# Implicit filters of two layers computed first on 128 partitions, and a thinner spread of the last eight channels' Haar work

## The chip, the cores and the metric

The kernel runs on one core of a Trainium2 chip. The metric is the device time of one execution in microseconds; each figure shown is a median of runs, and a profiled execution gives the trace that the text reads. TensorE does the matrix products, VectorE and ScalarE the elementwise work and the copies out of PSUM, and the queues of SyncE (SP) and ScalarE (ACT) issue all the transfers.

## The reference

Four layers follow each other on an input of 4 images, 64 channels, 256 x 256 pixels. Layers 0, 1 and 3 are long two-dimensional convolutions, one filter a channel, whose filter is the outer product of two vectors, `hx` and `hy`. Each vector comes from a small network:

```python
def _implicit_filter(z, w1, b1, w2, b2, w3, b3, wo, freq, t, deltas):
    h = jnp.sin(freq * (z @ w1 + b1))
    h = jnp.sin(freq * (h @ w2 + b2))
    h = jnp.sin(freq * (h @ w3 + b3))
    h = h @ wo
    return h * jnp.exp(-t * jnp.abs(deltas))
...
k = jnp.einsum('ijk,imk->ijmk', hx, hy)[0]        # one 256 x 256 filter a channel
y = irfft2(rfft2(x, 512) * rfft2(k, 512) / 512)[..., :L, :L]
out = y + x * bias[:, None, None]
```

`z` has 256 positions and 33 features, the hidden width is 64 and the output has one value a channel. So a layer needs two such networks, one an axis.

Layer 2 works in a Haar basis: a forward two-dimensional Haar transform, a scaling, a 64 x 64 mix of the channels, a soft threshold (twice, summed), the inverse transform, and the input added:

```python
f1 = haar2d(x)
for i in range(2):
    f4 = jnp.einsum('bchw,oc->bohw', f1 * v[i], conv_w[i])
    acc = acc + jnp.sign(f4) * relu(jnp.abs(f4) - tau[i])
y = haar2d(acc, inverse=True) + x
```

## The kernel before

**Convolutions as products.** Since a filter is separable, a convolution is a Toeplitz product from the left and one from the right. `contract` (lines 164 to 168) does one of them: four fp32 products of a 128 x 128 piece of the image with a piece of a Toeplitz matrix `t`. The Toeplitz matrix is not computed: `toeplitz` (line 155) loads it with a transfer whose rows overlap, from a padded copy of the filter that lies in DRAM (`pads`, one a layer). `first` (line 170) does one contraction and copies the result from PSUM with ScalarE into `a`; `second` (line 181) does the other, and VectorE adds the bias term into `y` (line 189).

**The filters** stand ahead of all this (lines 76 to 137). For each of 3 layers and 2 axes there are 3 steps: a product into `ps` on 64 partitions, then seven VectorE instructions that form the argument and reduce it into the range of the sine (lines 110 to 119), then ScalarE's Sin (line 121). An output product, a multiplication with the decay `dsb` and a transfer to `pads` follow (lines 123 to 132). Between them the tables of layer 2, `vts` and `fac`, are loaded, multiplied (line 134) and written to `scales` in DRAM (line 135). The constants of the Haar stages (`hbt`, `hb`, `hbr`, `hrow`) and of the mix (`wb`) are loaded at the very start.

**Four stages an image.** `convolutions(b)` loads an image's channel, does layers 0 and 1, and then the forward Haar transform: `pairs` (line 226) does the last `second` and the finest level of the rows into one of eight slots of `sd`; `levels` (line 234) does the other seven levels for four channels at once on VectorE, 14 instructions (lines 240, 241); `down` (line 254) does the columns as a product `pz` and writes `co` to `coef` in DRAM. For even channels (all of them in image 0) the operand of `pz` is first split into two parts, `sp`, by `split` (line 247: a ScalarE copy, line 251, and a VectorE subtraction, line 252). `mixing(b)` reads `coef` and does the mix and the threshold in 64 groups of rows, writing into the tile `z`, which fills most of the on-chip memory. `inverse(b)` transforms back, channel by channel: `fetch` (a ScalarE copy `zc` of `z`, a load `r`), `rows` (products `pw`, a ScalarE copy and a VectorE subtraction into `w`), `cols` (products `pu`, then `t` and `u` on VectorE), and `last`, which is layer 3's convolution. Every third channel of images 0 to 2 is put off: its `u` goes to DRAM (`late`), and its layer 3 is done under the last image's mixing.

**The order of the work** is written out by hand. Each stage of each unit is put down with a tick and a place in it (`at`, line 205), and at the end the events are sorted by tick and place and issued (line 447); the scheduler beneath can still move an instruction within what its own estimate allows. A convolution takes one channel a tick in image 0. The convolutions of image b + 1 are spread over the mixing of image b and two ticks more (`spread`, line 425), so that the last channels' Haar work falls into the first ticks of the inverse stage of image b. The tick at which that stage starts is called the border here; there are three of them. The next mixing starts when the inverse is done and all Haar work is at least three ticks old (line 445).

**Buffers that matter.** Toeplitz matrices have five buffers, `sp` one, `co` two, the PSUM tiles of all contractions and Haar products four banks. The filter stage has its own pool, which is released before the other pools are opened.

Of the kernel before, what the change touches and what calls it, by code (L numbers as in the profile page):

```python
# [20 lines left out]
GT = 4  # L21
# [16 lines left out]
def conv_seq_kernel(ctx, tc, x, fz, fw, bias, decay, haar, haar_row, factors, vt, taut, wmix, out):  # L38
# [20 lines left out]
    hbt = const.tile([P, P], F32, name="hbt")  # L59
    hb = const.tile([P, P], F32R, name="hb")  # L60
    hbr = const.tile([P, P], F32R, name="hbr")
    hrow = const.tile([P, 2, P], F32, name="hrow")
    nc.sync.dma_start(hbt, haar[0])
    nc.sync.dma_start(hrow, haar_row)
    hsinv, ident = hrow[:, 0, :], hrow[:, 1, :]
    wb = const.tile([P, 2, P], F32, name="wb")
    nc.vector.memset(wb, 0.0)
    for r in range(2):
        nc.sync.dma_start(wb[r * C : (r + 1) * C, r, :], wmix)
    bsb = const.tile([P, 3, C], F32, name="bsb")  # L70
    nc.sync.dma_start(bsb, ap(bias, 0, [[0, P], [C, 3], [1, C]]))


    scales = dram.tile([S // 4 // GT, P, 2, GT, 16], F32, name="scales")
    pads = [dram.tile([C, 2, ROW], F32, name=f"pad{layer}") for layer in range(3)]
    with tc.tile_pool(name="filt", bufs=2) as fp, tc.tile_pool(name="fps", bufs=4, space=PSUM) as fps:
        signs = fp.tile([P, P], F32, name="signs", bufs=1)
        nc.sync.dma_start(signs, haar[1])
        nc.scalar.copy(hb, signs)
        nc.scalar.copy(hbr, hbt)  # L80
        vts = fp.tile([P, 2, S // 4, 16], F32, name="vts", bufs=1)
        nc.scalar.dma_start(vts[:, 0], vt)
        nc.scalar.dma_start(vts[:, 1], taut)
        fac = fp.tile([P, 2, S // 4, 16], F32, name="fac", bufs=1)
        nc.scalar.dma_start(fac, factors)
        dsb = fp.tile([C, S], F32, name="dsb", bufs=1)
        nc.sync.dma_start(dsb, decay)
        zs, ws = [], []
        for layer in range(3):
            z = fp.tile([EMB, S + 2 * ORD], F32, name=f"z{layer}", tag="z", bufs=3)  # L90
            nc.sync.dma_start(z, fz[layer])
            w = fp.tile([ORD, 2, 3 * ORD + 4], F32, name=f"w{layer}", tag="w", bufs=3)
            nc.sync.dma_start(w, fw[layer])
            zs.append(z)
            ws.append(w)
        cur = {}
        both = [(layer, axis) for layer in range(3) for axis in range(2)]
        for step in range(3):
            for layer, axis in both:
                z, w = zs[layer], ws[layer]  # L100
                ps = fps.tile([ORD, S], F32, name=f"fp{step}_{layer}_{axis}", tag="fps")
                if step == 0:
                    nc.tensor.matmul(ps, z[:, S + axis * ORD : S + (axis + 1) * ORD], z[:, :S], start=True, stop=True)
                else:
                    nc.tensor.matmul(
                        ps, w[:, axis, (step - 1) * ORD : step * ORD], cur[layer, axis], start=True, stop=True
                    )
                par = 3 * ORD
                u = fp.tile([ORD, S], F32, name=f"u{step}_{layer}_{axis}", tag="u", bufs=3)
                nc.vector.tensor_scalar(  # L110
                    u, ps, w[:, axis, par + step : par + step + 1], w[:, axis, par + 3 : par + 4], ALU.add, ALU.mult
                )

# [3 lines left out]
                for c in (C1, C2, C3):  # L117
                    nc.vector.scalar_tensor_tensor(u, k, -c, u, ALU.mult, ALU.add)
# [440 lines left out]
```

## Time and profile before

| | |
|---|---|
| median of 3 runs | 3047.55 us (3045.93 to 3049.37) |
| profiled execution | 3052.63 us |
| span of its trace | 3050.6 us |
| TensorE busy | 2971.9 us, 97% |
| VectorE busy | 2518.7 us, 83% |
| ScalarE busy | 2117.0 us, 69% |
| moved by transfers | 649.36 MB, 213 GB/s |
| mean granted TensorE clock | 0.998 |

All times in a profile count from the start of the span. In a list of groups a row has the line, the engine, the operation, the tiles it writes and reads, the shapes and the count; behind the bar stand the busy time in us and the mean of one in ns, and behind the second bar the time for which the engine had been idle just before, with what ended it. In a timeline a row has the start in us, the duration in us, and then the same names; square brackets hold the idle time before it and what ended that. An fp32 product shows as two matmul records. In a list of windows a row has the stretch, its length, the busy time of TensorE, of its weight loads (PEld), of VectorE, ScalarE and GpSimd with the number of instructions, then the granted TensorE clock, the share of the DMA engines and GB/s.

### The profile page before, as it was taken

The numbers are of one execution on the slowest core, as the hardware profiler recorded it, in microseconds if no ns is written. First come the engines' busy times: TensorE is split into PE (matmuls) and PEld (weight loads), VectorE is DVE, ScalarE is ACT, GpSimd is POOL, SyncE is SP. The second block draws the span as 40 slices with busy tenths as digits, with TensorE's granted clock in tenths as the row PEclk, the third lists the DMA queues.
The fourth block names the chain that finished last, engine by engine and source line by source line (L and its number), as shares of the span: only waits on it lengthen the run. The fifth ranks groups of instructions, "written<-read, shape, count | busy, mean of one in ns | idle before, by whom it ended". The sixth has DMA issues, their size and how long they took to land. (4 is left out here: it accounts for less than half of the span.)

```text
span 3050.6 us, 51749 instructions
## 1 busy us (share of the span) xinstructions
PE 2971.9 (97%) x16944; PEld 2615.0 (86%) x16944; DVE 2518.7 (83%) x4549; ACT 2117.0 (69%) x4918; POOL 0.2 (0%) x4
## 2 busy tenths in 40 slices
PE   5999999999999999999999999999999999999999
PEld 2999988888888888888887888888887888888998
DVE  5667768999987878898987878899986889998776
ACT  1333336899885658888885658888885668887554
POOL 0000000000000000000000000000000000000000
PEclk9999999999999999999999999999999999999999
DMA  3777787666667776666667776666667777877776
GB/s 109 215 231 228 233 232 212 199 205 204 200 201 223 237 229 194 206 206 204 202 209 227 239 228 197 207 206 206 203 207 213 242 234 234 235 231 216 212 210 188
DMA packets 562239, 649.36 MB, mean 213 GB/s; under 512 B 44369, under 2 KB 447156, under 8 KB 561844
## 3 DMA queue, kind: packets, MB, share of 16 engines
q1 hardware_dynamic: 445972, 493.18, 56.6%
q10 hardware_dynamic: 116000, 152.87, 14.0%
q8 instruction: 137, 2.24, 0.3%
q14 instruction: 130, 1.06, 0.1%
HBM read 426.40 MB, written 219.48 MB: 212 GB/s over the span
## 5 line engine op out<-in xcount | busy, mean ns | idle before, releaser
L167 PE MATMUL py<-t,a 128*128 128x256 f32 x3072 | 924.5, 383 | 16.6 <-ACT a L176 11.1
L176 ACT COPY a<-pa 128x512 f32<-128x512 f32 x768 | 475.5, 621 | 464.5 <-PE pa L168 352.9
L327 ACT ACTIVATE f<-px,vt 128x64 f32<-128x64 f32 x2688 | 585.0, 348 | 103.2 <-DVE f L325 102.7
L168 PEld LDWEIGHTS py<-t,a 128*128 128x128 f32 x3072 | 584.0, 190 | 79.5
L168 PE MATMUL py<-t,a 128*128 128x128 f32 x3072 | 590.5, 274 | 0.0
L167 PEld LDWEIGHTS py<-t,a 128*128 128x128 f32 x3072 | 491.0, 191 | 89.7 <-issue 32.8
L308 PE MATMUL px<-wb,f 128*128 128x256 f32 x2048 | 499.4, 381 | 7.8 <-ACT f L327 6.8
L308 PEld LDWEIGHTS px<-wb,f 128*128 128x128 f32 x2048 | 364.5, 190 | 54.5 <-ACT f L327 17.8
L335 DVE TENSOR_TENSOR mag<-mag,vt 128x1024 f32<-128x1024 f32 x256 | 312.5, 1221 | 52.8 <-ACT mag L333 51.8
L167 PE MATMUL pa<-t,x 128*128 128x256 f32 x1024 | 307.5, 382 | 9.8 <-DMA t<-pad 9.8
L340 DVE SCALAR_TENSOR_TENSOR mag<-mag,f 128x1024 f32<-128x1024 f32 x256 | 312.0, 1219 | 1.1
L167 PE MATMUL pa<-t,y 128*128 128x256 f32 x1024 | 306.6, 381 | 1.3 <-DVE y L189 1.1
L371 ACT CAST w<-pw 128x512 fp32r<-128x512 f32 x256 | 150.2, 587 | 217.8 <-PE pw L369 208.5
L333 ACT ACTIVATE mag<-f 128x1024 f32<-128x1024 f32 x256 | 289.7, 1132 | 14.4 <-DVE z L344 6.8
L334 ACT ACTIVATE f<-f 128x1024 f32<-128x1024 f32 x256 | 278.7, 1088 | 27.0 <-DVE sd L231 15.6
L361 ACT COPY zc<-z 128x512 f32<-128x512 f32 x256 | 282.2, 1103 | 2.0 <-DVE z L344 0.8
L189 DVE SCALAR_TENSOR_TENSOR y<-x,bsb,py 128x512 f32<-128x512 f32 x256 | 190.4, 744 | 69.2 <-PE py L168 62.3
L385 DVE SCALAR_TENSOR_TENSOR t<-r,pu 128x512 f32<-128x512 f32 x256 | 175.5, 686 | 83.9 <-PE pu L381 76.7
L167 PE MATMUL pa<-t,u 128*128 128x256 f32 x772 | 236.2, 388 | 2.1 <-DVE u L389 1.4
L189 DVE SCALAR_TENSOR_TENSOR y<-y,bsb,py 128x512 f32<-128x512 f32 x256 | 190.3, 743 | 53.2 <-PE py L168 51.8
L189 DVE SCALAR_TENSOR_TENSOR y<-u,bsb,py 128x512 f32<-128x512 f32 x193 | 144.0, 746 | 103.9 <-PE py L168 101.4
L168 PEld LDWEIGHTS pa<-t,x 128*128 128x128 f32 x1024 | 195.7, 191 | 26.8
(65 smaller groups left out, 4430.5 us busy)
## 6 DMA issues: line engine op xcount, KB each, us to landing
t<-pad SPq DMA_DIRECT2D x768, 256.0 KB, 3.9
x<-in_x SPq DMA_DIRECT2D x256, 256.0 KB, 3.8
keep<-sd ACTq DMA_DIRECT2D x256, 256.0 KB, 3.1
coef<-co SPq DMA_DIRECT2D x256, 256.0 KB, 3.4
f<-coef SPq DMA_DIRECT2D x256, 256.0 KB, 3.9
r<-keep SPq DMA_DIRECT2D x256, 256.0 KB, 3.1
out_y<-y ACTq DMA_DIRECT2D x256, 256.0 KB, 3.6
late<-u ACTq DMA_DIRECT2D x63, 256.0 KB, 2.6
```

The lines of the kernel that those rows point to most:

```text
L167: nc.tensor.matmul(ps[:, m, :], src[:, 0, m * P : (m + 1) * P], t[:, ::-1], start=True, stop=False)
L168: nc.tensor.matmul(ps[:, m, P:], src[:, 1, m * P : (m + 1) * P], t[:, : P - 1 : -1], start=False, stop=True)
L176: nc.scalar.copy(a, ps)
L189: nc.vector.scalar_tensor_tensor(y, s[res], bsb[:, layer, c : c + 1], ps, ALU.mult, ALU.add)
L308: nc.tensor.matmul(ps[:, h, q, :], f[:, q, h * P : (h + 1) * P], wb.rearrange("p r n -> p (r n)"), start=True, stop=True,)
L327: nc.scalar.mul(f4[:, j], px[:, j], scale(g, 0)[:, j : j + 1])
L333: nc.scalar.activation(mag, f4, AF.Abs)
L334: nc.scalar.activation(f4, f4, AF.Sign)
L335: nc.vector.tensor_sub(mag, mag, over(g, 1, 16))
L340: nc.vector.scalar_tensor_tensor(mag, mag, 0.0, st[g]["f4"], ALU.max, ALU.mult)
L361: nc.scalar.copy(a, z[:, :, :, c].rearrange("p h (i k) -> p h k i", k=2))
L385: nc.vector.scalar_tensor_tensor(t, st[c]["r"], 0.5, ps, ALU.mult, ALU.add)
```

## The change

Two things change.

The filters: the two axes of a layer sit side by side on 128 partitions, with weights that are block diagonal (zeros elsewhere), so that a layer has three steps and not six. Only layers 0 and 1 are computed ahead of everything. After each of them a few products are issued whose results nobody reads (`warm`: 6 after the first, 9 after the second). The constants, the third layer's filter and the tables of layer 2 become events of ticks 4 to 17 in the first image's convolutions. All of these use parts of the tile `z` as their room, since it is empty until the first mixing; the filter pool is gone. Each pad is written by two queues, one axis each. The loads at the start are issued in another order: the filters' inputs first.

The border: an event of Haar work that belongs to the last two groups of four channels and whose tick is at or beyond the border is moved from border + k to border + 3k.

```diff
-    with tc.tile_pool(name="filt", bufs=2) as fp, tc.tile_pool(name="fps", bufs=4, space=PSUM) as fps:
...
-        for step in range(3):
-            for layer, axis in both:
...
-                nc.vector.tensor_scalar(k, u, INV_2PI, MAGIC, ALU.mult, ALU.add)
...
+    room = z.rearrange("p h r c -> p (h r c)")
...
+    dsb = part(S + 1)
+    def filters(layer, queue):
+        fz_sb, fw_sb = part(S + P, EMB), part(3 * P + 4)
...
+        def load():
+            nc.sync.dma_start(fz_sb, fz[layer])
+            queue.dma_start(fw_sb, fw[layer])
+        def begin(n):
+            ps = bank(f"fp{layer}_{n}").rearrange("p m s -> p (m s)")[:, :S]
+            if n == 0:
+                nc.tensor.matmul(ps, fz_sb[:, S:], fz_sb[:, :S], start=True, stop=True)
+            else:
+                nc.tensor.matmul(ps, fw_sb[:, (n - 1) * P : n * P], st["h"], start=True, stop=True)
+            u, k = st["u"], st["k"] = part(S), part(S)
+            nc.vector.tensor_scalar(
+                u, ps, fw_sb[:, par + n : par + n + 1], fw_sb[:, par + 3 : par + 4], ALU.add, ALU.mult
+            )
+            nc.vector.tensor_scalar(k, u, INV_2PI, MAGIC, ALU.mult, ALU.add)
+            nc.vector.tensor_scalar(k, k, -MAGIC, None, ALU.add)
+        def finish(n):
+            u, k, h = st["u"], st["k"], part(S)
+            for c in (C1, C2, C3):
+                nc.vector.scalar_tensor_tensor(u, k, -c, u, ALU.mult, ALU.add)
+            nc.vector.tensor_scalar(u, u, PI_IN, -PI_IN, ALU.min, ALU.max)
+            nc.scalar.activation(h, u, AF.Sin)
+            st["h"] = h
+        def end():
...
+            nc.vector.scalar_tensor_tensor(f[:, :S], ps, dsb[:, S:], dsb[:, :S], ALU.mult, ALU.mult)
+            for axis, queue in enumerate((nc.scalar, nc.sync)):
+                queue.dma_start(pads[layer][:, axis, :], f[axis * C : (axis + 1) * C])
+            st["f"] = f
+        def warm(n):
+            ps = psx.tile([P, 2, S], F32, name=f"warm{layer}", tag="mix")
+            for i in range(n):
+                nc.tensor.matmul(ps[:, i % 2, :], st["f"][:, :P], st["f"][:, :S], start=True, stop=True)
...
+    def constants():
+        signs = part(P)
+        nc.sync.dma_start(hbt, haar[0])
+        nc.sync.dma_start(signs, haar[1])
+        nc.sync.dma_start(hrow, haar_row)
...
+        nc.scalar.copy(hb, signs)
+        nc.scalar.copy(hbr, hbt)
+    def tables():
...
+        def load():
+            nc.sync.dma_start(vts[:, 0], vt)
+            nc.sync.dma_start(vts[:, 1], taut)
+            nc.sync.dma_start(fac, factors)
+        def scale(i):
+            nc.vector.tensor_mul(vts[:, i], vts[:, i], fac[:, i])
+            nc.sync.dma_start(
+                scales[:, :, i].rearrange("n p g j -> p n (g j)"), vts[:, i].rearrange("p (n g) j -> p n (g j)", g=GT)
+            )
...
-    def convolutions(b, ticks, in_parts=()):
+    def convolutions(b, ticks, in_parts=(), border=None):
+        def after(tick, n):
+            return tick if border is None or tick < border or n < C // 4 - 2 else border + 3 * (tick - border)
...
             for s, steps in enumerate([(1,), (2, 4), (8, 16, 32, 64)]):
-                at(end + 1 + s, 1, levels(steps), n)
+                at(after(end + 1 + s, n), 1, levels(steps), n)
             for j in range(4):
                 if 4 * n + j in in_parts:
-                    at(end + 3 + j, 2, split, 4 * n + j)
-                at(end + 4 + j, 2, down, 4 * n + j)
-        return ticks[-1] + 11
+                    at(after(end + 3 + j, n), 2, split, 4 * n + j)
+                at(after(end + 4 + j, n), 2, down, 4 * n + j)
+        return after(ticks[-1] + 11, C // 4 - 1)
...
+    one, two, three = filters(0, nc.scalar), filters(1, nc.scalar), filters(2, nc.sync)
+    one[0]()
+    nc.sync.dma_start(dsb, decay)
+    two[0]()
+    nc.sync.dma_start(bsb, ap(bias, 0, [[0, P], [C, 3], [1, C]]))
+    for do in (one[1], one[2], two[1], one[3], one[4], two[2], one[5], one[6], two[3], one[7], *two[4:7]):
+        do()
+    one[8](6)
+    two[7]()
+    two[8](9)
+    for tick, do in enumerate([constants, None, None, *three[:-1], *tables()], 4):
+        if do is not None:
+            at(tick, 3, lambda unit, do=do: do(), 0)
...
-            ready = convolutions(b + 1, spread(ahead, end + 2), in_parts=range(0, C, 2))
+            ready = convolutions(b + 1, spread(ahead, end + 2), in_parts=range(0, C, 2), border=end)
```

On the host, the decay gets a second copy of its rows (one an axis) and a column of scale factors, and each layer's weights are laid out block diagonally.

## The prediction

> **What bounds it now.** I read the page first: busy shares and slices.
>
> ```profile
> PE 2971.9 (97%) x16944; PEld 2615.0 (86%) x16944; DVE 2518.7 (83%) x4549; ACT 2117.0 (69%) x4918; POOL 0.2 (0%) x4
> PE   5999999999999999999999999999999999999999
> ```
>
> TensorE is busy for 2971.9 of 3050.6 us, so the time is its work plus its idle 78.7 us, of which the first slice holds about half. Work that is only moved on another engine is worth nothing; idle or slow TensorE time that is removed is worth all of itself. So I went to the timeline of the start, TensorE alone.
>
> ```profile
> 47.25 1.94 PE L126 MATMUL fo<-h,w 64*64 64x256 f32 x4 [2.07 <-DVE f L129]
> 58.94 1.19 PE L167 MATMUL pa<-t,x 128*128 128x256 f32 x2 [9.75 <-DMA t<-pad]
> ...
> 66.51 1.06 PE L167 MATMUL pa<-t,x 128*128 128x256 f32 x2
> ...
> 68.73 0.60 PE L167 MATMUL pa<-t,y 128*128 128x256 f32 x2
> ```
>
> The first useful product starts at 58.94 us, and until about 68.4 every pair takes 1.06 us, afterwards 0.60: TensorE runs at half rate for 9.4 us (starts are 0.43 us apart where they are 0.22 later). What fills the 58.94 us is in the groups by line:
>
> ```profile
> L118 DVE SCALAR_TENSOR_TENSOR u<-k,u 64x256 f32<-64x256 f32 x54 | 20.0, 406 | 0.0
> L110 DVE TENSOR_SCALAR u<-fp,w 64x256 f32<-64x256 f32 x18 | 9.5, 527 | 8.1 <-PE fp L103 8.1
> L121 ACT ACTIVATE h<-u 64x256 f32<-64x256 f32 x18 | 7.5, 417 | 30.7 <-DVE u L119 30.7
> ```
>
> Eighteen filter steps (3 layers, 2 axes, 3 steps) of seven VectorE instructions; in the timeline two steps take 4.13 us (9.53 to 13.66), so 18 take 37 us, one after another. Then I looked for the other idle time, in windows at the three borders where an inverse stage begins while the next image's convolutions end (columns: stretch, length, then each engine's busy time).
>
> ```profile
> 949.00:956.00 7.00, 3.64 (x19) 2.43 (x17) 6.87 (x21) 3.21 (x4) 0.00 (x0) 0.99 0.70 218
> 956.00:963.00 7.00, 6.32 (x21) 5.44 (x22) 3.25 (x6) 3.57 (x6) 0.00 (x0) 0.52 0.26 93
> ...
> 1643.00:1650.00 7.00, 3.69 (x21) 2.72 (x19) 6.43 (x20) 3.65 (x5) 0.00 (x0) 1.00 0.69 223
> ...
> 2335.00:2342.00 7.00, 3.58 (x20) 2.62 (x18) 6.12 (x20) 2.93 (x4) 0.00 (x0) 0.97 0.69 220
> 2342.00:2349.00 7.00, 6.15 (x21) 5.25 (x22) 3.40 (x7) 3.49 (x6) 0.00 (x0) 0.54 0.35 107
> 970.00:1045.00 75.00, 75.00 (x473) 66.44 (x473) 61.62 (x119) 50.97 (x70) 0.00 (x0) 1.00 0.77 240
> ```
>
> Each border has 7 us in which TensorE is busy 3.6 us and VectorE 6.1 to 6.9; after two of them the granted clock is 0.52 and 0.54. The last line, the quiet rest of the inverse stage, shows TensorE full and VectorE at 82%. The timeline names the wait:
>
> ```profile
> 955.80 0.17 DVE L241 SCALAR_TENSOR_TENSOR sd<-sd 128x8 f32<-128x8 f32 x1
> 956.01 0.62 ACT L251 CAST sp<-sd 128x512 fp32r<-128x512 f32 x1 [1.65 <-DVE sd L241]
> 956.66 0.69 DVE L252 TENSOR_TENSOR sp<-sd,sp 128x512 fp32r<-128x512 f32 x1 [0.68 <-ACT sp L251]
> 956.68 0.79 PE L259 MATMUL pz<-sp,hbr 128*128 128x512 f32 x1 [2.94 <-ACT sp L251]
> ```
>
> The product `pz` of channel 60 waits for its split `sp`, which waits for the Haar levels of channels 60 to 63 on an overfull VectorE; the rows and columns of the inverse stand behind it in TensorE's order.
>
> [...] here 9.4 us went by at the start, and a drop lasts nearly 7 us (0.52 over 7 us). [...] The trace of before shows no large load just ahead of a small urgent write; the change makes one.
>
> **The change, part by part.**
>
> *Filters, removed.* Both axes share 128 partitions: 9 steps for 18. Rows don't cost: 128x256 additions (L389) take 0.42 us, 64x256 ones (L118) 0.41. Layer three's 3 steps go into the first convolutions' ticks, so 6 stand ahead. They are now a chain of latencies. Steps: 1.15 us from a product's start to VectorE's read (8.38 to 9.53); seven dependent instructions alone 0.54+0.28+0.28+3x0.41+0.27 = 2.6, with gaps estimated 2.8; two layers interleaved 4.13; from Sin's start to the next product 0.86 (13.43 to 14.29).
> First operand lands at about 3.9 (now `hbt`, issued at 0.73, ends a wait at 4.27); VectorE from 5.05; layer one's step ends at 8.9. But ScalarE's queue holds `hbr<-hbt` and the Sin table load (1.28) ahead of the first Sin, and `hbt` is now issued behind three 256 KB loads of x (5.7 us to landing): about 8.9+0.3+1.28 = 10.5. Then product 11.35, VectorE 12.5, Sin 15.3, product 16.2, VectorE 17.3, with layer two's second step interleaved to 21.5, output product 22.35, filter written 23.9. Layer two: last step 24.4 to 27.2, output product after the six warm products (0.86 each, cold) at 29.2, filter 30.75. Nine warm products follow: 3.9 us at full rate, 7.7 at half; taking the middle, the convolutions start at **36.8**, mostly warm.
> Data: the pad write of layer one goes out at 24 but behind a 512 KB load of `vt`, issued just ahead of it on SP (4.0 us to landing at the start), so about 28; the Toeplitz load takes 4.3: 32.4, before 36.8. Layer two's: 30.8+2.85+4.3 = 38, needed about 4.6 us after the start, 41. So the warm products, not the loads, set the start; without that cover it would be 33 to 38.
> Before, 9.4 us at half rate are worth 4.7 at full, so the full-rate start was 58.94+4.7 = 63.6. Gain 63.6-36.8 = **26.8 us**, bounds 20 (all cold, loads late) to 31.
>
> *Layer three, constants, tables, moved* into ticks 4 to 17 of the first convolutions. TensorE pays four products of 0.44: **-1.75**. VectorE gets 3x2.07+0.5 and two multiplications of 1.2, 9 us, ScalarE 3 Sins of 0.42 and two casts; VectorE was busy 180 of 260 us there (200 to 460), so the cover is its 31% of idle time; uncovered it is 9 us. SP's queue gets 512 KB and 1 MB loads, two 512 KB writes and a pad in front of Toeplitz loads, with the DMA engines at 0.78. The 1 MB load took 5.2 us; a Toeplitz load (five buffers, two taken per tick of 5.24, each held about two ticks) is issued some 1.5 ticks, 7.9 us, ahead of use and takes 3.9, so it may be 1 us late. I take **-1** for both, bounds 0 and -6.
>
> *The border.* The last eight channels' products leave ticks 3 to 13 and come every third tick until 36; stage starts don't move (the next mixing starts 64 ticks after the border). Price of the stall: idle 3.36+3.31+3.42 = 10.1 us, and two half-rate stretches of about 6.8, worth 3.4 each: 16.9. In the built order channel 60's product now stands 18 ticks later, so its wait goes. What is late next: VectorE. One group's levels are 5.2 us; the built order spreads them over six ticks instead of four, not eighteen. A quiet tick is 2.86 us (21 in 60), VectorE 82% of it, 0.5 spare: six ticks absorb 3 of 5.9 us (a split of 0.69 added). The 2.9 left delay `u` and `w`, for which TensorE waits beyond a stage's slack: between 0 and 2.9 us per border; I take 1. Gain 16.9-3 = **13.9**, bounds 16.9 and 1.4 (2.9 each and the half rate back). ScalarE's `co` and `sp` (0.6 us each) come with the products; ScalarE's 68% in the quiet windows (50.97 of 75) hides them.
>
> Sum: 26.8-1.75-1+13.9 = **38.0 us**. Span 3050.6-38.0 = 3012.6; the profiled execution's 2.0 us around it make 3014.6. That execution (3052.63) lies 5.1 above the median, so against the median I say 3047.55-38 = **3009.5**.
>
> **Rivals.**
> *The border only moves its stall* (start gain alone): for it, VectorE's levels are hardly spread in the built order; against, the waiting product is far away. 3047.6-24.1-1.4 = 3022.
> *The start gives back a dozen microseconds*: loads late behind tables, convolutions starting cold. [...] Start 12 instead of 24: 3022; with a better border 3019.
> *Slower: the spread makes VectorE the bound over 36 ticks after each border.* It has 0.36 us per tick more (13 us over 36), ScalarE 0.4. If each delays the chain rows, `w`, columns, `u` by its whole length, 0.76 us x 108 ticks = 82 us; it turns the result from 0.41 us per tick (38+6 over 108), that is a VectorE tick of some 3.4 us where I count 2.35+0.36 = 2.7. At 0.5: 3063.
> *No effect*: the chain of filters being shorter is plain in the built order; only chance cancelling would do it.
>
> **How the numbers follow.** Forecast 0.68; border moved 0.13; start given back 0.11; slower 0.06; no effect 0.02. Its own range is 2999 to 3017 (start 20 to 31, border 10 to 17). The first two rivals lie within 3025, the best bounds (31 and 16.9, less 1.75) at 3001, with clock drops differing by run 2997. Faster by over 0.2% (about what a measurement here can tell from none) 0.92, within 0.02, slower 0.06.
>
> **What would show it.** Right: first `pa` near 37 us, its pairs at 0.60 from the start; no wait of `pz` for `sp` over 1 us at the borders and no half-rate stretch after them; quiet inverse windows still full. Wrong: `pa` after 43 or at 1.06; waits `pa` for `t` in the first 150 us; idle TensorE with `u` L389 or `w` as releaser through ticks 3 to 36.

## The result and the profile after

| | before | after |
|---|---|---|
| median of the runs made side by side | 3047.62 us (4 runs) | 3008.99 us (3003.69 to 3010.56, 4 runs) |
| ratio, 95% interval | | 0.987 (0.9853 to 0.9887) |
| profiled execution | 3052.63 us | 3009.79 us |
| span of its trace | 3050.6 us | 3007.9 us |
| TensorE busy | 2971.9 us | 2952.9 us |

The change makes the kernel 38.6 us faster. The forecast was 3009.5. From the page of the kernel after, busy shares and slices (engine, time, share, instructions; then TensorE's busy tenths in 40 slices):

```profile
PE 2952.9 (98%) x16950; PEld 2613.0 (87%) x16950; DVE 2498.9 (83%) x4480; ACT 2112.8 (70%) x4909; POOL 0.2 (0%) x4
PE   7999999999999999999999999999999999999999
```

TensorE's idle time has gone from 78.7 us to 55.0 (3007.9 less 2952.9), and its busy time has fallen by 19 us. Products at half rate last longer (a pair 1.06 us against 0.60), and after the start there are none of these left in the body of the trace; the filters' own products took 22.9 us before and 11.1 now, and the warm products add 8.2.

**The start.** From the timeline of the kernel after (start, length, engine, line, what it writes, count, and in brackets the idle time before it with what ended it):

```profile
9.61 0.30 ACT L156 CAST hbr<-hbt 128x128 fp32r<-128x128 f32 x1 [6.68 <-DMA hbt<-in_haar]
9.93 1.28 ACT L125 ACT_TABLE_LOAD   x1
11.22 0.72 ACT L125 ACTIVATE z<-z 128x256 f32<-128x256 f32 x2
...
22.56 1.22 PE L130 MATMUL fo<-z 128*128 128x256 f32 x2 [4.11 <-ACT z L125]
...
24.43 4.04 PE L142 MATMUL warm<-z 128*128 128x256 f32 x12
...
28.07 0.90 SPq L180 DMA_DIRECT2D t<-pad  x2
...
29.48 4.15 PE L142 MATMUL warm<-z 128*128 128x256 f32 x18 [0.58 <-DVE z L133]
...
33.48 0.59 PE L189 MATMUL pa<-t,x 128*128 128x256 f32 x2
```

The first Sin is held by the cast of a Haar constant and by a table load, the first output product comes at 22.56, the Toeplitz load can be issued at 28.07, and the convolutions start at 33.48 us (58.94 before) with pairs of 0.59: at full rate. The clock had become full at 26.9, during the first batch of warm products (24.43 to 28.47).

**The borders.** Windows of the kernel after at the three borders and in the quiet rest of an inverse stage (stretch, length, busy time of TensorE, weight loads, VectorE, ScalarE, GpSimd, then granted clock, share of the DMA engines, GB/s):

```profile
919.00:926.00 7.00, 6.56 (x43) 5.74 (x42) 6.50 (x14) 3.93 (x6) 0.00 (x0) 1.00 0.71 196
926.00:933.00 7.00, 6.08 (x39) 5.28 (x38) 6.93 (x15) 5.62 (x8) 0.00 (x0) 1.00 0.87 274
...
949.00:1024.00 75.00, 75.00 (x472) 66.90 (x471) 61.56 (x118) 52.96 (x75) 0.00 (x0) 1.00 0.83 252
1612.00:1619.00 7.00, 6.47 (x42) 5.62 (x41) 6.97 (x15) 5.32 (x7) 0.00 (x0) 1.00 0.78 241
2297.00:2304.00 7.00, 6.46 (x41) 5.57 (x41) 6.92 (x15) 5.05 (x7) 0.00 (x0) 1.00 0.85 244
```

The windows that had 3.6 busy microseconds in 7 now have 6.1 to 6.6, the clock is 1.00, and the quiet rest is as full as it was (75.00 of 75), though it now carries the moved work.

**What was given back.** The first convolutions, which lost nothing before, now lose time. Windows of the kernel after, and its timeline in them:

```profile
110.00:120.00 10.00, 8.25 (x47) 7.02 (x46) 5.59 (x10) 2.18 (x4) 0.00 (x0) 1.00 0.95 300
120.00:130.00 10.00, 9.50 (x56) 8.37 (x55) 8.95 (x23) 4.36 (x8) 0.00 (x0) 1.00 0.93 251
130.00:140.00 10.00, 9.09 (x54) 8.13 (x53) 3.77 (x7) 3.77 (x7) 0.00 (x0) 1.00 0.96 268
```

```profile
114.43 1.23 DVE L170 TENSOR_TENSOR z<-z 128x1024 f32<-128x1024 f32 x1 [4.41 <-DMA z<-in_factors]
...
116.68 0.67 PE L189 MATMUL pa<-t,x 128*128 128x256 f32 x2 [1.74 <-issue]
...
133.69 0.67 PE L189 MATMUL pa<-t,y 128*128 128x256 f32 x2 [0.91 <-DMA t<-pad]
```

VectorE waits 4.41 us for the 1 MB load of `fac`, the DMA engines are 93 to 96% busy, and TensorE waits for Toeplitz matrices. The list names no cause ("issue") for the wait that ends at 116.68, but a Toeplitz load issued at 107.97, 2.57 us behind that of `fac`, landed at 116.59.

**Where the time went, by stretch.** Both traces hold the same products in the same order within each name, so the start of the k-th `pa` (or `px`, `pw`) in one trace less that in the other is a shift, and its change over a stretch is what that stretch won (negative) or lost. The table gives these changes in us against the trace of before, for this kernel and for those of the experiments. "Start" ends with channel 3's first product, "channels 3 to 32" with channel 32's, "to border 1" with the 500th record of `px`; each border's column reaches well into the mixing after it.

| kernel | start | channels 3 to 32 | to border 1 | border 1 | border 2 | border 3 | whole |
|---|---|---|---|---|---|---|---|
| after | -29.7 | +7.9 | +1.4 | -7.0 | -6.4 | -8.9 | -42.7 |
| start only | -30.0 | +8.4 | -0.3 | -1.5 | +1.4 | -3.6 | -25.7 |
| border only | -1.0 | +0.1 | -2.0 | -8.8 | -6.8 | -8.8 | -27.2 |
| levels left | -29.1 | +7.1 | -0.5 | -3.5 | -3.5 | -7.0 | -36.5 |
| every second tick | -30.1 | +6.7 | +0.4 | -4.1 | -3.4 | -5.1 | -35.6 |
| every fifth tick | -29.2 | +6.5 | -0.2 | -0.2 | -2.2 | -3.7 | -29.1 |
| third tick, one later | -30.1 | +7.6 | -0.9 | +2.8 | +4.4 | +0.3 | -15.8 |
| no warm products | -28.3 | +7.1 | -2.1 | -9.5 | -7.6 | -8.1 | -48.4 |
| multiplications later | -30.0 | +6.4 | -1.8 | -6.7 | -3.0 | -8.7 | -43.9 |
| tables spread | -29.6 | +3.2 | +0.4 | -10.4 | -6.8 | -7.7 | -50.8 |
| tables on GpSimd | -30.1 | +6.3 | -1.4 | -6.7 | -6.7 | -9.1 | -47.6 |
| five warm products | -33.9 | +2.4 | +3.8 | -8.0 | -6.7 | -9.7 | -52.1 |
| three warm products | -34.4 | +2.6 | -0.2 | -7.5 | -6.3 | -10.2 | -56.0 |

The whole is some 5 us more than the medians say, because the profiled execution of before lies 5 us above its median. Stretches that no edit touches differ by up to 4 us from trace to trace, also where the clock did not drop (among kernels that are alike there, "to border 1" goes from -2.1 to +1.4 and border 1 from -10.4 to -6.7), so single differences of that size mean nothing.

### The profile page after: what moved, and what is told of

Read it like the earlier page. It is cut to its first block, busy times and chain, and to the rows that moved or that the text cites. A ratio compares the mean times of both kernels' runs of the same rounds, so it can differ in the third digit from the quotient of the medians.

```text
span 3007.9 us, 51671 instructions
## 1 busy us (share of the span) xinstructions
PE 2952.9 (98%) x16950; PEld 2613.0 (87%) x16950; DVE 2498.9 (83%) x4480; ACT 2112.8 (70%) x4909; POOL 0.2 (0%) x4
## 3 DMA queue, kind: packets, MB, share of 16 engines
q14 instruction: 130, 1.06, 0.1%
```

## The experiments

My theory after the result: the two parts add; the start is worth what it was forecast to be or a little more, the transfers of the tables give some of it back, and the border is worth more than forecast. Rivals: the border is worth 14 and something else makes up the rest; VectorE, not the transfers, gives the start's part back; the warm products do nothing.

### The border undone

```diff
-            ready = convolutions(b + 1, spread(ahead, end + 2), in_parts=range(0, C, 2), border=end)
+            ready = convolutions(b + 1, spread(ahead, end + 2), in_parts=range(0, C, 2))
```

> The changed kernel with the border undone (Haar work of the last eight channels at its old ticks), filters as changed. Theory A (the two parts add, and the border is worth more than the 13.9 us forecast, because the whole stretch of 20 to 25 us around each stall falls short, 21.5 us together): 20 to 25 us slower than the changed kernel, about 3031 us, and at each border the wait of the product for its split and the half-rate stretch are back. Theory B (the border is worth the forecast 13.9 us, the rest of the shift seen there belongs to the different phase of the clock): 12 to 16 us slower, about 3023 us. Theory C (the start gave most of the gain, the border only moved its stall): under 5 us slower.

Measured: 3027.85 us (3024.84 to 3032.55), ratio to before 0.9939 (0.9924 to 0.9954). That is 18.9 us above the changed kernel, between theories A and B. The waits are back. Timeline at its first border:

```profile
933.88 0.62 ACT L277 CAST sp<-sd 128x512 fp32r<-128x512 f32 x1 [1.65 <-DVE sd L267]
934.53 0.69 DVE L278 TENSOR_TENSOR sp<-sd,sp 128x512 fp32r<-128x512 f32 x1 [0.69 <-ACT sp L277]
...
934.55 0.50 PE L285 MATMUL pz<-sp,hbr 128*128 128x512 f32 x1 [2.95 <-ACT sp L277]
```

and its windows at the first border and at the second:

```profile
926.00:933.00 7.00, 4.47 (x23) 3.09 (x21) 7.00 (x18) 3.78 (x5) 0.00 (x0) 1.00 0.68 218
...
1627.00:1634.00 7.00, 7.00 (x35) 5.87 (x34) 3.46 (x7) 3.31 (x6) 0.00 (x0) 0.81 0.35 120
```

Nearly the same wait (2.95, 2.81 and 3.18 us) is followed by no half rate at the first border and by one stretch of about 3.4 us at the second and third (granted clock 0.95 and 0.81 in two windows of 7 us, and 0.76 in one). In the kernel before, the stretches were 6.827 us (the trace's record of the clock), twice that, at borders 1 and 3, and there was none at border 2. So half rate came on top of a stall or did not, and cost up to 3.4 us each time, half of 6.827; the last section has TensorE's busy time at some of these stalls. This may be why the border is worth 18.9 us against this run and, in the next experiment, 21.9 against the kernel before, whose trace has the longer stretches.

### The border alone

The kernel before, with `border=end` and the function `after` put in as in the change.

> The kernel before with nothing but the border's every third tick. Theory A (the parts add): 3024 to 3028 us, which is 20 to 24 us less than before, and its start is that of before to the first mixing (first convolution product at 59 us, half rate for 9.4 us). Theory B (the border is worth 13.9): 3034 us. If the parts interact, what this run and the one with the start alone gain does not sum to the whole gain of 38.6.

Measured: 3025.17 us (3024.71 to 3027.27), ratio 0.993 (0.9915 to 0.9945): 21.9 us below the runs of before made beside it (3047.11). Theory A holds, within the runs' spread: 21.9 and, from the start alone, 19.3 make 41.2 against 38.6 for both. Windows of this kernel at the three borders (columns as above):

```profile
940.00:947.00 7.00, 6.26 (x41) 5.49 (x40) 6.88 (x14) 3.96 (x5) 0.00 (x0) 1.00 0.67 193
...
1625.00:1632.00 7.00, 6.48 (x43) 5.68 (x42) 6.95 (x14) 3.89 (x5) 0.00 (x0) 1.00 0.65 177
2310.00:2317.00 7.00, 6.38 (x42) 5.60 (x41) 6.85 (x14) 3.96 (x5) 0.00 (x0) 1.00 0.59 185
```

VectorE is as full there as before (6.9 of 7), yet TensorE works 6.3 to 6.5 us instead of 3.6: what this part of the change took away is the product's early place in TensorE's order, not VectorE's load in the first ticks.

### Levels left where they were

```diff
-                at(after(end + 1 + s, n), 1, levels(steps), n)
+                at(end + 1 + s, 1, levels(steps), n)
```

> The changed kernel, but the Haar levels of channels 56 to 63 stay at their old ticks; only the splits and the column products come at every third tick. Theory A (the stall is TensorE's order: the product stands in the queue before its split can be ready; VectorE's overfull ticks by themselves cost little): nearly all of the border's gain stays, within 3 us of the changed kernel. Theory B (VectorE is overfull for some 7 us at each border and delays the inverse's own operands w and u whoever is queued): 3 to 9 us slower than the changed kernel, with TensorE waiting for w or u in the first six ticks after each border.

Measured: 3012.64 us (3011.52 to 3016.0), ratio 0.9889 (0.9875 to 0.9904): 3.7 us above the changed kernel, at the seam of the two theories, and the intervals overlap (0.9853 to 0.9887 for the changed one). The products' order makes most of the gain; spreading the levels adds a few microseconds at most. The waits for `w` and `u` that theory B names are there, but small: at borders 2 and 3, TensorE's waits ahead of `pu` and `pa` sum to about 1 us more each than in the changed kernel. The half-rate stretch in this trace (at 892.05) follows a wait of 2.26 us for `y` at the first tick of the inverse stage; the kernel with the multiplications later has one of 2.23 us there, with the levels spread, so it does not come from this edit.

### Every second and every fifth tick

```diff
-            return tick if border is None or ... else border + 3 * (tick - border)
+            return tick if border is None or ... else border + 2 * (tick - border)
```

and the same with 5.

> The changed kernel with the Haar work of the last eight channels at every second tick instead of every third. Theory A (any order in which the product is a few ticks behind its split removes the stall): within 2 us of the changed kernel. Theory B (VectorE's spare time per tick sets what is left, 0.5 us in a tick of 2.86): the added work per tick is half as much again, so 3 to 6 us slower, with TensorE waiting for u and w between ticks 3 and 25.

> The changed kernel with the Haar work of the last eight channels at every fifth tick. Theory A (what every second tick lost, 9 us, was VectorE's and ScalarE's spare time per tick, and every third tick still pays part of it): 1 to 4 us faster than the changed kernel. Theory B (every third tick is spread enough; what is left at a border, 3 us each, comes from the convolutions' own end in the first six ticks): within 1.5 us of the changed kernel. Theory C (the last products now end so late that they collide with the loads of the next mixing): slower.

Measured: every second tick 3018.02 us (3016.88 to 3020.48), ratio 0.9908 (0.9891 to 0.9924); every fifth tick 3019.75 us (3017.21 to 3023.44), ratio 0.991 (0.9893 to 0.9926). Both are some 10 us slower than every third tick. The first is worse than theory B allowed, and a thinner spread made it no better, against A and B of the second. More spare time a tick is not what counts. In the trace of every fifth tick the losses are not at the next mixing's loads either (theory C), but, at the first border, in single products of `pa` that start 0.7 to 1.2 us late because their `u`, of ticks 27, 48 and 57 of the inverse, is late: all multiples of three. That pointed to the next experiment.

### Every third tick, one tick later

```diff
-            return tick if border is None or ... else border + 3 * (tick - border)
+            return tick if border is None or ... else border + 3 * (tick - border) + 1
```

> The changed kernel with the Haar work of the last eight channels still at every third tick, but one tick later, so that it meets another third of the inverse's channels. Every third channel's layer three is put off, so the inverse's own work has a period of three ticks; in the changed kernel every such product stands in the same tick of it, and loses nothing, while at every second and every fifth tick the products walk through all three and the losses (0.7 to 1.2 us at a time) come one tick on from the others. Theory A (which tick of the three the Haar work meets is what made every second and fifth tick slow): 4 to 12 us slower than the changed kernel. Theory B (it is the spacing): within 2 us of it.

Measured: 3038.52 us (3036.67 to 3042.77), ratio 0.9974 (0.9962 to 0.9985). One tick later costs 29.5 us: more than theory A's 12, and more than leaving the border alone (3027.85). Groups of TensorE by line in 105 us after the first border, first in this kernel (935 to 1040 us), then in the changed one (count, busy time, mean ns, idle time before them and what ended it):

```profile
L189 PE MATMUL pa<-t,u 128*128 128x256 f32 x86 | 26.4, 389 | 5.9 <-issue 3.2 <-PE pu L407 2.8
...
L394 PE MATMUL pw<-hrow,zc 128*128 128x128 f32 x124 | 22.7, 278 | 1.2 <-DVE y L211 1.2
```

```profile
L189 PE MATMUL pa<-t,u 128*128 128x256 f32 x92 | 27.8, 384 | 0.0
...
L394 PE MATMUL pw<-hrow,zc 128*128 128x128 f32 x138 | 24.8, 275 | 0.0
```

In the changed kernel TensorE does not wait once in this stretch. What VectorE and ScalarE wait for, in the chain of waits of this kernel over the same 105 us (waiting instruction, what ended the wait, us in total, times, longest):

```profile
DVE y L211 <- DMA out_y<-y: 6.5, 7, 1.5
```

```profile
ACT co L293 <- DMA late<-u: 8.3, 4, 2.3
```

Neither wait exists in the changed kernel between 930 and 1035 us. And from VectorE's timeline at one of the stalls, this kernel first, then the changed one at the same kind of tick:

```profile
996.93 0.68 DVE L411 SCALAR_TENSOR_TENSOR t<-r,pu 128x512 f32<-128x512 f32 x1
997.52 0.68 DVE L278 TENSOR_TENSOR sp<-sd,sp 128x512 fp32r<-128x512 f32 x1
998.12 0.42 DVE L414 TENSOR_TENSOR u<-t 128x256 f32<-128x256 f32 x1
```

```profile
993.75 0.68 DVE L411 SCALAR_TENSOR_TENSOR t<-r,pu 128x512 f32<-128x512 f32 x1
994.46 0.43 DVE L414 TENSOR_TENSOR u<-t 128x256 f32<-128x256 f32 x1
```

Layer three of every third channel is put off, so the inverse's own work has a period of three ticks, and one tick in three has no `py` product and no `y` of layer three. In the trace of the changed kernel all Haar products stand in this tick (after `pa`, ahead of `pw`); one tick later they stand behind a `py`. There the split's subtraction comes between `t` and `u` on VectorE, and `co`, which shares its two buffers with layer three's `y` (tag "co" in `down` and in `last`), meets that `y`: the wait of `y` for `out_y` is a wait for such a buffer. That the tick matters is shown, of two ticks out of three: two ticks later was not tried. That the buffers and the subtraction are the ways in which it works is read from these waits; neither was tried by itself, and why `co` waits for `late` is left open.

### No warm products

```diff
-    one[8](6)
     two[7]()
-    two[8](9)
```

> The changed kernel without its fifteen warm products ahead of the convolutions (they compute nothing that is used). Theory A (the clock is full at the first convolution because of them): the first convolution product starts at 31 to 32 us instead of 33.5, when its Toeplitz matrix lands, but its pairs take 1.06 us instead of 0.60 for 3.4 to 10 us, which costs 2 to 5 us; net 0 to 3 us slower than the changed kernel, seen best in where channel 6 starts. Theory B (the filter products have warmed the clock enough, the warm products only stand in the way): 2 us faster.

Measured: 3003.81 us (3003.58 to 3010.17), ratio 0.9858 (0.9844 to 0.9871), which overlaps the changed kernel's. In the place that the edit touches, the timeline of TensorE at its start:

```profile
31.68 1.19 PE L189 MATMUL pa<-t,x 128*128 128x256 f32 x2 [2.20 <-issue]
...
37.98 1.06 PE L189 MATMUL pa<-t,x 128*128 128x256 f32 x2
...
39.11 0.60 PE L189 MATMUL pa<-t,x 128*128 128x256 f32 x2
```

It starts 1.8 us sooner, at half rate until 38.95, and channel 3, from where both run alike, starts 1.4 us later than in the changed kernel (-28.3 against -29.7): theory A, at the low end. The run's median is 5.2 us better than the changed kernel's, but in the traces that comes from stretches that the edit does not reach (border 1 and "to border 1" are 6 us better), so it says nothing on the warm products; what is said of them here rests on the start of one trace each.

### What the tables cost

Three kernels take the given-back time apart: the multiplications alone moved, the loads spread as well, and the same transfers on another queue. In the first two each late instruction is held at its tick by a copy of one element from that tick's data, which it then overwrites; in the second the four loads are `vt`, `taut` and two halves of `factors`, and the last two ticks are those of the multiplications.

```diff
+    for tick, do in zip((22, 24), scale):
+        at(tick, 3, lambda unit, do=do: do(), 0)
...
+            nc.vector.tensor_copy(out[:, i, 0, :1], sd[:, 4 * i, 0, 0, :1])
-            nc.vector.tensor_mul(vts[:, i], vts[:, i], fac[:, i])
+            nc.vector.tensor_mul(out[:, i], vts[:, i], fac[:, i])
```

> The changed kernel with the loads of the tables where they are, but the two multiplications and their writes at ticks 22 and 24 (into a place of their own). Theory A (4.5 us of what the start gives back in ticks 15 to 18 is VectorE held by the multiplication that waits for the 1 MB load): 2.5 to 4.5 us of it are back; the idle time at 114.7 us (1.9) is gone. Theory B (it is the transfers, 1.5 MB of loads in front of Toeplitz loads): the stalls stay where they are, under 1 us back. In both, the write of 512 KB may cost 0.5 us at its new place.

```diff
-        def load():
-            nc.sync.dma_start(vts[:, 0], vt)
-            nc.sync.dma_start(vts[:, 1], taut)
-            nc.sync.dma_start(fac, factors)
+        def load(to, src, slot):
+            nc.vector.tensor_copy(to[:, 0, :1], sd[:, slot, 0, 0, :1])
+            nc.sync.dma_start(to, src)
...
+    for tick, do in zip((20, 24, 28, 32, 32, 40), tables()):
+        at(tick, 3, lambda unit, do=do: do(), 0)
```

> The changed kernel with the tables in four loads of 512 KB at ticks 20 to 32 and the multiplications at ticks 32 and 40, each load and multiplication held by a copy of one element. Theory A (VectorE's wait is the cause): as with the later multiplications alone, about 3 to 4.5 us back against the changed kernel. Theory B (transfers): 3 to 4.5 us back here and under 1 us there. Both leave layer three's 3.4 us (four products 1.7, stalls 1.7). The load of the first table is also gone from ahead of the first filter's write, so that this write should land about 1 us sooner; the first convolution stays at 33.5, behind the warm products.

```diff
-            nc.sync.dma_start(vts[:, 0], vt)
-            nc.sync.dma_start(vts[:, 1], taut)
-            nc.sync.dma_start(fac, factors)
+            nc.gpsimd.dma_start(vts[:, 0], vt)
+            nc.gpsimd.dma_start(vts[:, 1], taut)
+            nc.gpsimd.dma_start(fac, factors)
...
-            nc.sync.dma_start(
+            nc.gpsimd.dma_start(
                 scales[:, :, i].rearrange("n p g j -> p n (g j)"), vts[:, i].rearrange("p (n g) j -> p n (g j)", g=GT)
```

> The changed kernel with nothing but another queue for the tables: their three loads and two writes go out on GpSimd's queue instead of SyncE's; sizes, ticks and the multiplications are the same. Theory A (SyncE's queue stands still[...]): the stalls of ticks 15 to 18 shrink from 4.5 us to under 2. Theory B (the DMA engines are simply full, whichever queue the bytes come from): 4 us or more stay. In both, the multiplication still waits for its load on VectorE.

Measured: multiplications later 3007.14 us (3005.21 to 3009.27), ratio 0.9864 (0.985 to 0.9877); tables spread 3002.86 us (3001.53 to 3006.23), ratio 0.9851 (0.9838 to 0.9865); tables on GpSimd's queue 3005.86 us (3002.82 to 3012.6), ratio 0.987 (0.9855 to 0.9885). The times of the first and third are within the noise of the changed kernel's; the shifts from channel 12 to channel 32 are sharper: lost there 4.9 us in the changed kernel, 3.5 with the multiplications later, 4.2 on GpSimd's queue, and 0.7 with the loads spread (each with one product of layer three, 0.43, in it). The spread transfers reach to tick 40, though, and that kernel loses 1.3 us more by channel 48, where the other three lose nothing: 3.0 of the 4.9 us are back. So the transfers' size and place is the cause. VectorE's wait for the multiplication is not: with the multiplication moved away, other work of VectorE waited there for a transfer, 5.28 us for `keep`. VectorE and TensorE with the multiplications later:

```profile
114.95 0.69 DVE L268 TENSOR_TENSOR sd<-sd 128x512 f32<-128x512 f32 x1 [5.28 <-DMA keep<-sd]
```

```profile
116.21 0.67 PE L191 MATMUL pa<-t,x 128*128 128x256 f32 x2 [1.62 <-issue]
```

and TensorE with the tables on GpSimd's queue, and the windows with the loads spread:

```profile
115.05 0.67 PE L189 MATMUL pa<-t,x 128*128 128x256 f32 x2 [1.40 <-DMA t<-pad]
```

```profile
110.00:120.00 10.00, 10.00 (x61) 9.13 (x60) 7.94 (x20) 4.35 (x8) 0.00 (x0) 1.00 0.72 219
...
130.00:140.00 10.00, 10.00 (x61) 9.12 (x60) 7.47 (x16) 3.82 (x8) 0.00 (x0) 1.00 0.72 210
```

TensorE's wait ends when a Toeplitz matrix lands: with the multiplications later at 116.12 us, for the product at 116.21; on GpSimd's queue at 114.91, for the one at 115.05; and in the changed kernel at 116.59, for the one at 116.68. So it is TensorE's own operand that is late, whatever VectorE waits for. A Toeplitz load took up to 8.6 us to land in the changed kernel between 105 and 125 us, up to 9.4 between 95 and 140 on the other queue, and with the loads spread at most 4.5 between 105 and 125, where no table moves any more, and 6.4 between 136 and 225, where the tables do. Changing the queue left 4.2 of 4.9 us. Theory A of the third run (SyncE's order) fell, and theory A of the first two fell in its larger half; the 1.4 us that the later multiplications got back may be the writes, which moved with them.

### A version that beats both

The Sin table is loaded ahead of everything by a Sin of one zero, the Haar constant and its cast are taken out of `constants` and go ahead of the images, on ScalarE's queue, the tables are spread, and there are five warm products instead of nine after the second filter:

```diff
+    seed = part(1)
+    nc.vector.memset(seed, 0.0)
+    nc.scalar.activation(seed, seed, AF.Sin)
     one[0]()
     nc.sync.dma_start(dsb, decay)
     two[0]()
+    nc.scalar.dma_start(hbt, haar[0])
+    nc.scalar.copy(hbr, hbt)
...
-    two[8](9)
+    two[8](5)
```

> The changed kernel with the tables spread, a Sin of one zero as the first thing on ScalarE (so that its table load is over before the filters), the Haar constant loaded on ScalarE's queue ahead of the images, and five warm products instead of nine after the second filter. Theory A (the chain of the filters and the warm products set the start, and the tables the give-back): first Sin at 9.1 instead of 11.2, first convolution at 28.5 to 30 instead of 33.5 and still at full rate; 3.5 to 5 us there and 3 to 4.5 from the tables: 6.5 to 9.5 us less than the changed kernel, about 3001 us. Theory B (the landing of the first two filters' Toeplitz loads sets the start): first convolution not before 31.4, about 3004 us. Theory C (five warm products are too few): it starts at half rate, no gain at the start.

Measured: 2998.23 us (2996.15 to 3001.13), ratio 0.9834 (0.982 to 0.9847). The first Sin is at 8.95 us and the first convolution at 29.34, at full rate (theory A; B and C fall). But 3.9 us were lost between channels 32 and 34 of the first image. SyncE's queue and TensorE there, from the timeline:

```profile
200.48 0.34 SPq L165 DMA_DIRECT2D z<-in_factors  x1
...
202.34 0.36 SPq L173 DMA_DIRECT2D scales<-z  x1
203.52 4.62 SPq L296 DMA_DIRECT2D coef<-co  x1
...
214.44 0.69 PE L191 MATMUL pa<-t,x 128*128 128x256 f32 x2 [2.02 <-DMA t<-pad]
```

A 512 KB load and a 512 KB write in one tick: the next issue takes 4.62 us instead of 0.36, the Toeplitz loads behind it are late, TensorE waits 2.02 us, and a half-rate stretch of about 3.4 us follows (granted clock 0.66 from 215 to 220 us). The kernel with the tables spread has the same pair in its tick 32:

```profile
208.71 3.49 SPq L298 DMA_DIRECT2D coef<-co  x1
```

There TensorE waited 0.52 us, no half rate followed, and 0.8 us were lost between channels 30 and 36. So the pair makes a Toeplitz load late, and by how much differs from run to run. I put the multiplications and writes in four halves at ticks 38, 44, 50 and 56, and took three warm products:

```diff
-    two[8](5)
+    two[8](3)
-    for tick, do in zip((20, 24, 28, 32, 32, 40), tables()):
+    for tick, do in zip((20, 24, 28, 32, 38, 44, 50, 56), tables()):
```

> The kernel with the early Sin, the tables in four loads at ticks 20 to 32, now multiplied and written in four halves at ticks 38 to 56, away from the loads, and three warm products after the second filter. Theory A (the 3.9 us lost at 215 us in the version with five warm products came from a 512 KB load and a 512 KB write in one tick): these are back and the first convolution starts 0.9 us sooner: about 4 us less than that version, 2994 us. Theory B (the writes cost wherever they are): no more than 1 us. Theory C (three warm products let the clock fall): the first convolutions run at half rate and cost 2 us.

Measured: 2996.06 us (2994.71 to 2999.76), ratio 0.983 (0.9815 to 0.9844): 12.9 us below the changed kernel. From channel 3 to the 500th `px`, 2.4 us are lost instead of 6.2, as theory A has it; the time moved by only 2.2 us against the version with five warm products, within the runs' spread. The first convolution is at full rate (theory C falls), 0.5 us sooner and not 0.9:

```profile
27.43 1.56 PE L142 MATMUL warm<-z 128*128 128x256 f32 x6 [0.58 <-DVE z L133]
28.83 0.59 PE L193 MATMUL pa<-t,x 128*128 128x256 f32 x2
```

A table load takes 1.28 us here. The changed kernel, whose first ScalarE work is a copy, loads a table twice; this one, with the Sin first, loads one, and no copy that follows in it loads another.

## Why the prediction was right, point by point

The time was right to within a microsecond, and the chosen case was the one that happened: both parts gain, and the tables give a little back. That the sum came so close is luck. Of its four terms one was on the spot and three were off by 3 to 8 us, in both directions, and two of these three lie outside the bounds that I gave for them.

- **Start, 26.8 us.** The traces show 29.7 by channel 3. The chain of latencies held: output product 22.35 against 22.56, first filter written at 23.9 against 24.3, layer one's Toeplitz load issued at 28 and 28.07. That its filter's write lands late behind the load of `vt` was an estimate; it landed 3.5 us after its issue, layer two's, with no table ahead of it, after 2.9. What was mis-sized is the warm products: "3.9 us at full rate, 7.7 at half; taking the middle". The clock was full at 26.9, while the first six still ran, and the nine took 4.15. Layer two's filter was also 1.3 us sooner than forecast (29.42 instead of 30.75), and the convolutions started at 33.48 instead of 36.8. The step "the warm products, not the loads, set the start" is borne out: without them it is 31.68.
- **Layer three on TensorE, 1.75 us.** Four steps of 0.43 in the shifts.
- **Layer three and tables, 1 us, bounds 0 and 6.** The step that failed is that a Toeplitz load is issued "7.9 us, ahead of use and takes 3.9, so it may be 1 us late". Issued 2.57 us behind the 1 MB load of `fac`, one took 8.6 us. Stalls were 6.2 us between channels 3 and 32 (7.9 less the four products), just outside the bound: about 4.5 from the tables, 1.7 while layer three's work was on VectorE. The rival "the start gives back a dozen" had the cause right, loads behind tables, but twice the size: 6.2 us of stalls, not a dozen. One of the signs that I had named for being wrong, `pa` waiting for `t` in the first 150 us, did show.
- **Border, 13.9 us, bounds 1.4 and 16.9.** Measured 18.9 against the kernel with the start alone, 21.9 against before. That the wait of channel 60's product would go was right. The idle time was mis-sized: I took it from one window of 7 us a border, 10.1 us, and added 6.8 for half rate. Counting, for each product, how much later than usual the next one starts, the kernel before loses about 10.6, 8.1 and 12.0 us around the three borders, and the changed one 3.6, 2.9 and 3.7: a few waits of about 1 us ahead of the stall and behind it belong to it. Some stay: `py` waits for `y` 0.96, 0.97 and 1.43 us at the first tick of the three inverse stages before, and 1.12, 0.97 and 1.42 after. The 1 us a border that I retained was low by about two, and the removed loss low by twice that.
- **The slower rival.** It was ruled out by averages (VectorE 2.7 us of work in a tick of 2.86). One tick later, with the same averages, the border loses 29.5 us: waits of `u` up to 1.2 us come one after another, as the rival had it. That the changed kernel doesn't pay them comes from the tick that its Haar work falls into, which my working did not look at: the 0.06 was too low for the reasons that I gave.
- **The half-rate stretches, about 6.8 us each.** They are 6.827 us in the trace of before, at borders 1 and 3, and about 3.4 at borders 2 and 3 of the kernel with the start alone. The price of one trace's stalls thus holds for that trace: what a stall adds at half rate differs from trace to trace (last section).

## What to carry to other kernels

Before moving work between stages that repeat, write down the period of the work that it will meet and what each tick of it leaves free, on engines and in shared buffers: the same work at the same spacing won 19 us in one tick of three and lost 11 in the next. Price a stall by the products' start-to-start distances over the whole stretch, not by the idle time of its worst window. Large loads that nobody waits for yet still have to be cut up and spread: here small urgent ones landed late behind them with the tables on SyncE's queue (up to 8.6 us) and on GpSimd's (up to 9.4).

## What was not expected of the hardware

- Stalls of nearly the same length were followed by half rate in one place and not in another. From the kernel before: the 3.42 us ahead of the fall of the clock at border 1 and the half rate after it, a stretch of that length at the stall of border 2, after which the clock did not fall, and the 3.42 us ahead of the fall at border 3, with TensorE's busy time behind the length:

```profile
952.41:955.83 3.42, 1.32 (x8) 1.03 (x7) 3.32 (x13) 0.59 (x1) 0.00 (x0) 1.00 0.63 184
955.83:959.24 3.41, 2.56 (x9) 2.29 (x10) 0.84 (x2) 0.86 (x2) 0.00 (x0) 0.50 0.14 53
959.24:962.65 3.41, 3.41 (x11) 2.86 (x11) 2.56 (x5) 2.36 (x5) 0.00 (x0) 0.50 0.35 124
...
1645.32:1648.73 3.41, 1.60 (x9) 1.28 (x8) 3.41 (x12) 1.33 (x2) 0.00 (x0) 1.00 0.67 222
...
2338.22:2341.64 3.42, 0.93 (x7) 0.69 (x5) 3.13 (x10) 0.59 (x1) 0.00 (x0) 1.00 0.46 143
```

- Two such stretches from the kernel with the start alone (at the stalls of borders 1 and 2) and one from that with the multiplications later:

```profile
929.96:933.37 3.41, 1.57 (x8) 1.28 (x8) 3.38 (x12) 0.68 (x2) 0.00 (x0) 1.00 0.53 173
1622.88:1626.30 3.42, 0.79 (x6) 0.55 (x4) 2.83 (x11) 1.08 (x2) 0.00 (x0) 1.00 0.58 185
1863.16:1866.58 3.42, 1.50 (x10) 1.24 (x9) 2.72 (x10) 3.42 (x12) 0.00 (x0) 1.00 0.34 120
```

- After the second and the third of these (busy for 0.79 and 1.50 us) the clock fell, after the first (1.57 us) it did not. The wait of TensorE was 2.95 us at border 1, 2.81 at border 2 and 1.92 in the third: the longest was not followed by half rate, and the shortest was. What decides it these cases do not show. Half rate then lasted about 3.4 us at border 2 of the kernel with the start alone, and 6.827 us at borders 1 and 3 of the kernel before, where TensorE was busy for 2.56 and 2.20 of the first 3.41 us of it. In these traces a stall thus cost its length and up to 3.4 us. The stretches at half rate differ from trace to trace, which may be a part of why the runs of before range from 3042.8 to 3052.6 us; that was not tried.
- On the way up, the clock is full at 68.36 us in the kernel before, 9.4 us after the first convolution product, and 7.3 us after it without warm products. In the changed kernel TensorE is busy throughout from 23.51 to 26.93 us, with the filters' own products and the first warm ones, and the clock is full at 26.93, ahead of the first convolution.
- An issue on SyncE's queue behind a 512 KB write took 4.62 us in one kernel (five warm products) and 3.49 in another (tables spread), instead of 0.36.
